# A planned order with another length for a trip through DRAM, and a causal mask that moves from TensorE to GpSimd

## The chip, the cores and the metric

The kernel runs on one core of a Trainium2 chip. The metric is the device time of one execution in microseconds, the median of several runs. A core has five engines with a queue of instructions each: PE (TensorE, matmuls), DVE (VectorE), ACT (ScalarE), POOL (GpSimd) and SP (SyncE, which here only issues DMAs). Each engine takes its instructions in order, and waits at an instruction until the semaphores that it needs have been raised by others.

## The reference

The input x is 8 images of 56 x 56 tokens with 128 channels. Layer 0 is a deformable convolution: per token a depthwise 3x3 convolution gives offsets and weights for nine samples in four channel groups; the samples are summed, projected, and followed by a layer norm, an MLP of 512 and a second layer norm. Layer 1 is causal attention over the 3136 tokens of an image, and then a layer of 64 experts that each choose 8 tokens of an image. The part that the change touches is the attention:

```python
scores = jnp.einsum('bqu,bku->bqk', q, k) / jnp.sqrt(jnp.asarray(T, jnp.float32))
causal = jnp.tril(jnp.ones((T, T), dtype=jnp.float32))
scores = scores + NEG * (1.0 - causal)
attn = jax.nn.softmax(scores, axis=-1)
context = jnp.einsum('bqk,bku->bqu', attn, v)
```

A query sees the keys up to its own place; the softmax subtracts the largest score of its row before the exponential.

## The kernel before, in words

`local_kernel` computes everything. (A general version stands behind a flag for offsets that reach too far; its flag isn't set for these inputs.) The work is cut into 32 groups: 8 images of 4 groups of up to 7 tiles of 128 tokens (896 tokens, or 448 in one group of each image). For each group there is a chain of steps, each a Python generator: `bring` and `prepare` (load and transpose x), `conv`, `plan` (offsets to tap weights), `fetch` (DMA of the neighbourhood, tile g), `weigh` (DVE multiplies g by the taps), `sums` (POOL adds the 25 taps up; for image 0 partly PE), `back`, `project` (the projection, MLP and norms), and then the attention: `norm`, `scores`, `maxes`, `keyed`, `exps`, `attend`, `after`. At the end, behind all groups, stand the experts.

The scores of the attention are computed twice, because the two uses need them the other way round:

- `scores` (L975) makes them with the queries on the partitions (tiles sc). `maxes` (L995) takes each row's maximum on DVE, block by block, and negates it (L1005, L1007). The causal mask is added on the diagonal blocks by a small bf16 matmul of an identity with `maskq` (L990), accumulated into the same PSUM tile.
- The negated maxima stand one to a partition. They have to become one row: ACT issues a DMA of neg to a row in DRAM (L1013, L1017), and SP issues a DMA of that row into the first partition of qT, the transposed queries (L1019). The first channel of the normalised tokens is left free (it holds a one), so that the subtraction of the maximum is part of the next matmul.
- `keyed` (L1040) makes the second scores with the keys on the partitions (tiles st): the matmul at L1047, in pieces of up to 128 keys by 448 queries. A piece that cuts the diagonal has m > 0 columns to mask, and gets a second small matmul with `maskk`, the transposed mask (L1055). There are 803 pieces, and 224 of them are masked. PSUM tiles come from a ring of five (`gen`).
- `exps` (L1060) lets ACT take the exponential of a piece into pe, a ring of three SBUF tiles (L1068).
- `attend` (L1071) multiplies pe by the tokens (tiles av, L1079), accumulated over the keys of a block of queries.

An fp32 matmul is recorded as two instructions, so the 803 pieces appear as 1606.

The order in which the instructions are issued on every engine is fixed when the kernel is built. Each step yields `need(engine, us, ...)`: which engine it uses next, for how long, which ring slots it takes and gives, and with `since` from what time on it may start. These numbers served a planner that isn't part of the file; what it found is written out as the long string `ORDER` (L102 on), one letter a step (x is maxes, t is keyed, e is exps, a is attend, and so on). When the kernel is built, the loop at L1423 only reads a letter and lets that step issue its next instructions; of a `need` it uses the ring slots, for assertions, and nothing else. So an edit of a time in `need` changes nothing by itself; it takes effect through another `ORDER`.

The times that the planner had for the trip of the maxima through DRAM are in these lines of `maxes`: 4.0 us from the issue of the write to the issue of the read, and 2.6 us from there on to the row being in place.

```python
        at = yield need(SP, 0.1, since=at + 4.0)
        nc.sync.dma_start(qT[:1, :N], row[:N].rearrange("(o n) -> o n", o=1))
        yield need(DVE, 0.0, since=at + 2.6)
```

`keyed` and `exps` of a group may begin when `maxes` of that group is done.

Of the kernel before, what the change touches and what calls it, by code (L numbers as in the profile page):

```python
# [9 lines left out]
BF16 = mybir.dt.bfloat16  # L10
# [3 lines left out]
ALU = mybir.AluOpType  # L14
AX = mybir.AxisListType

P = 128
# [57 lines left out]
def need(engine, us, take=None, give=None, since=None, kind=None, when=None, lock=False):  # L75
# [27 lines left out]
    "ppppppbpbkppppbwpwwwpwpwpvkvfvvvvvvvwvpfpccpccwcpwwcbwccfcppccpcccwpcwpccpcbwcvcvcvcvcvcvccv"  # L103
    "cvvwggvvwsvwwvvvvwsvvvgfsvppcccspbccpgppbpscgcpfsscccspcpccvcfsscsvcvcvvcsmvcvcmvfvcvmcvcmvc"
    "vcvmmcvmcvmmvcvmcmvmmgmgvpbmpvgspcmpkscpvmgcfssmsmmmmmpssnpnnnnsfvncvncngpnnsnnncfspncvqqxqv"
    "qgvpgscccfxsscxxgxsvbvcssxvfccsvcgxcctscteftvstvevaevaeavacsvcvcvavocfpcospmccoompoocpcoppoc"
    "opbcbpmggcommoomosoccmococmmpomcmgcsmgmfmpmvcvcvssvcvcsoccccmfsssvcmgcmoscmgsmommfmvmvmcvsgc"
    "vmvcmskmvcmfsvmvmmgmmmcmscmcvvcvmfssvvovooopcgscpcpfssgmpcmgpppmsmmmkmpcfssnmnpgcmspmcmcfncs"
    "smncncmcnmgcscmnvcmfssnmmcmmgnsmnnvbmnvnfvnnvncgcssngcmncmnscnmvvcnfmssmmnmnmvmvnqmgcscvvkcc"
    "xqfsqxcvqmqxxqcmxqxqxcvqcxqcxbsmxqqmqxxmxqvmcmxqmvsvvvvmxfsvgpqpqcmmxgspmxmgxbmskcmpxgpmvcfs"  # L110
    "xtctectcmmcamcmsstesvcmvescvtsesvtsfcvtmtagaaeeameaevasmatatvestvenvtnsntsnnstnsfnentgvaaeae"
    "naeaevgasnvanvmntvnsnmtesctnsageseasfnatnemnacmnmsavonvmmsvnmcsmvnscvnmpcgnbmcpcvcvcoqcqxoxc"
    "qocqqcxoxcqxomxqksmsoqxfqxoqxoqxqxmoqxqxsmqxqmxcqmxsqxcqmmcqxcmxxqmqxoqxmoqxqosmoqqxoxqxqxqs"
    "xosxoqsfxomoxpmxopmgcmspmpmmosmmcxbgscvmsoscmsfocogxpttsetvtvsevaesaecvscmscvokamvfagomtcoet"
    "coamcmomtomseocseacoavostoposestssptfgetetppottsapnnannsanenpnbesnesttpntpgpabpsasfaepeeagpa"
    "etatespttvcstnvnavssavesnctfesangnteanntensvanvenvansvensvanssensfganqqqcqxcxqxqxqcxqxcxqcxq"
    "xcqxqxcqxgqccacaqqcxxcqxqcxqcxxqxqsgxcxqvcscqcsqxsvxqscxsfqxvqcxqccxqcxqsxvmqxmqxsvmxsqsvmsv"
    "qsfxqxtxtcectecsgtettsamaevaescmasvsagcfetcaetcqecqcvcqxqvxcqcxcxqcxmaxacmqcamcxcqgmmqmpobpx"
    "mxqompxopxmoppbmopomoooooxoompkmxotptemttommetmemtmptvavaevtevomvamvomevoavmavaomteetetootot"
    "ooaaemoaoaemeomemoammotmmoommotmoemooomakmaaemtmtmemtmsentnnmntnmsnannmestmtassaseamfetenmaa"  # L120
    "aetesnateanteannaesannanmgsntnstsesaesfnmtngnmnnstneaseqmqxsqxsqxssfqxqgqmamsamxxstxmmssqmsq"
    "xsfemgsxmqmstxkstemtetxsmtgssfaaeceagcsceavmmmcamsacxvsmctsvmsctvsfmgxcteteaesmavavetmcvaesv"
    "ctvsctsectsecftmctctavcaegcaeaecaevacamcapbmcpomocmmgpcmcmocmmtmcpmopccvcevvmvoktmoaootemote"
    "oteomamaematmsotaeomvtmsvemvvtsmvtstoasmaennnansmnasfnnnemeameaamanmmogcmmnmmsnmnccmsncncsnc"
    "snsvsfvovnmnvgnvnvosnvnvonvsvnksmqssqxfqcxmqxqxsqcxqxcmoqxoqmoxqoxsoqmxoqcxsmocxqvsmqsxsmxfq"
    "mcomxvcomvqqcomxqxqmcqxcmxqcxqxqmcxmcxqmcvmxcomvmxvpmcmvcbomovcmvocpvoxcooomcpkcpcxtgmttemet"
    "etpmmtmmsanaennaennnaesnnaagnottesntesoaesnasgnsfonantntteenaeatosteaoetosonoanososeonoasnos"
    "fonagnntnoqeqgxqxsoqoxqoxqoxsoqxosqxosqosxosfqxqxqxqxgmqsmmsqmqxxqssxsasfxagoqoosqoxqxmxqxqs"
    "mxqxsqsxmsqxsfmoxmogcmmsommoccsmomgsposmotbsosmfccgpsemqmqcqxxqkcmcxaxvsqmmqmsmscqmsqcxsfxcq"
    "xqxtxxtegstteaseaesqcsqcssfqxxtxtgxtetaspeaspaecpsaxcaesapsampsfnonnnnxtpeomapsogppmpstbstes"  # L130
    "bposesgftptegptavnaeavasnvnotontnosvenevtsevstnsvmsnfvtvangaeaecaecaoaocoqocooqxmqxocqmqcxxq"
    "xmcqmqcxqoxqxxqxqcoxocqxoqxoqxocomxsogqmmcqsmmocqxmsxqcoxqxqxsgcsxsfqvcvcqxoxtovtesvovtcosva"
    "evsoeavsoscavcsfcovctgoteteaecsavmccttsomtsecmscsooocfcegccpcqpcqcqxcpcxxcbapaemcqkapcxacmgc"
    "apqbmpttexpmxmaepampmtmvtevmvtmexvmvtmvttexvmavmavaeemaemmammammtmmtmememtkmttemamaemmaemsaa"
    "mstmtestetsesttsasfaeaeaeaamsanonmntsotsentmnenanensmasganftmeosnannotgntmeoetosnoanooemonos"
    "onmoomssagsnasfmnmnnmmnonmtnqqsoxqoxemxssogsososfomotqeoqxosqmxqxqxqmxkqxsomxaosmaxmsgossfto"
    "teocomgoscamoceosavooxmststsecsftcgtxetetvmasoavaecsevtevasccsvasevafcvacvmcvtmctctemgeamate"
    "tectetcvptbgcacetacaecmeamaecaapcmommocpcoptmcmocttomopomocotmomvevvcvecovcomakvmaataemotoma"
    "momomsevomvomvosnmeennonansmoansonaosomtntestmoanfeeanamaonnmnomnnsmmgcnmmnommcnscmngcmncovv"
    "cocvvsvcnovmnovkcnvonvoqscosqcxsqsmfxqxvqxqvxpoxqosqpoxqxqmxvqbxsqxmsqmxsqsxsfqxmqxpxqmmqxsm"  # L140
    "xqmpmpxsopmcsqbqscspqmxfxqcmqcpxcxmcxmxocmocmomcommocpommgoxomcpmcccoxtcvoectoctcevoteotooot"
    "oomoakmooaageoeaeamaootomtmomemstogaeotaesoaeotaetonsanteasonensanosnasnfnovmotvmovemnovovmt"
    "vsteteansaesnagsnasnsfntnteotnoaensoooatntseenstnsgtsensftnganeaneqmqxsmqxqxmsxqmqsxmsxsagms"
    "faaqeqqxsxaqxqxsaqxosxqsosqsfxoxqomxqmgsmqmmsqmsqxgsmxsxsfxgmscmoccsoqvckspsxqbpsmqocfxqxqmx"
    "qxqmqxxqxqmmpmsssxmxqmspsmxpsnfnpmnqnonqxnqpxqxqmxnoqnxmqxoqbxnmxnpoxmnonmgnmmnqmxmosoqmpmpq"
    "xxmtxoxtegttsoaetoesgaoeqsesqvsqsfoqomvgovovoocsxccxxqcxscvqcxqssxqxsqsfxcmtgmtamaetesctxakm"
    "somemaocsmaecosmcaogsmcfamomococmvqcqxocqoqmqxxqcmxqxcxqcxqxcqxtoooctcetxectvecgttsqaaevgqev"
    "axsxqeqxsmxcmssvcmscqsfqxmmxvamvxacsvacvttvetstevecasvaesmvxcsatsvfmmgtvxpmtcmscpccsaecbspsm"
    "spetkcppfgcamcaaemetcaemcmpacmmsampbmmpptsgmttstesteseasvsfaevaevavavtvmtvesvaemvatsmeststse"
    "gsftettamgasetetasaeaessaesasfatatnennaennannsnototnegteoetcnntcntcnocancnagnsenonasesnsansf"  # L150
    "eonoaonoonoomonocqmqcxqcxcqxqoxqxqxqsxoqoxoqxosmxooagsmsmosscfommoxcomcomcvscvgcsvcxvssvtcsv"
    "tsfevtexgtectctsctavaevsmvesakmcsacsfacemtgeaevaapcopmtcmmtcbemmpctpocageoceaocpaovctocvmvtm"
    "cevmcevtmvtcvtectvacvaeomaeaecomoaatomatmeoemoammaommotommoototmoemoeeoomaokatmaaomtotommeme"
    "omseanonmnnomnsntonnmeontmotoaaseaeomaanasmossosnfmnmonnmonnmosnomooonsoommonosgcnsmsnsfmnnm"
    "ccngqcvscmvxovovvmvsqkmqcqsxxqxomqxoqxosmoqsxosfqmoxqoxcqmxqxcmqsxcqmcqxcsxqoqxosxmsxqmscfmx"
    "qcmqcqxmxqxmqxqxoxmovxomvmocmmvcovcmmgmmxmcvpbmcpccgxovoctoctectgcpemetkcmtcvacvaecvtepamopp"
    "abemmpammsanmnnpmnoootsteptsnptntmnsensetsmvsfavaveaevaeatantveaetstentntsntnsngassannmfeaea"
    "smanemnamensagnntnsnestsnsgqesfqaaqxsxqxqqxxsqxqxssqxsqxsfqxqxqxtxsgteteteqsqqssxaxssfmexgcm"
    "mqmmsqcmxgcxsmcscqmsqcsxcsfmxgcccscmqcmcsqqkcvmxaxpsmabmsapqmsmqmsfxmxpmxmancqmqsxqxqxmnqxqx"
    "smpqnqsnpsnqxnqxqxsxnqcfxnmnxcqxnnxpcmxoncgmpcncmmpmconmxcbqcgmmcomxtsteomgessqpgqsxpqsxsvxq"  # L160
    "sfxqxqxqxvoaoacootocootceootceoaexmovakmvagtmtetesaeoqmmosqxomqosxoqsxosmqsofxqoxqoxvqxqxqsv"
    "qxxaxsqvosmqsoxsmxsofmgmoqmoqomqxsqmxqxxmsqxmqsxmsxsamgsfmcmmommcgstcmvotvsxtovtsvsomevssfvv"
    "egemamasaeacmootccxktsevtesvtsevstctfavxaevmtemvmamsagsaettseatesteascmscpsfmctcpmgtmpsaaeps"
    "apcbasecepsabpssafgtepettseptgptstvmavaevsavessvaesfgaemaattcevstevaveavcastctesgctesaecsasf"
    "attemeamatactnenoncenctnncntecnacoaenagamcncnomcmscogmmcscmmsvcscomstcfsvtcvtvmvcvcsvcocecsm"
    "ectkesmctsctsoancofoaeomvntevsanmnvtemagnneanseavaoasoonotntgontenasesnesmcafmnmoqqoxcqxoqoc"
    "xocpxqpcqxqxcopbocoqpcqxopcoxaoxtvgcoectcoaceovqovovtotoeteooottxavxmeavmtvemvtvmtaaemxaemaa"
    "emeamxatameommommoamoomotomotoemoeoomoakmattotmeotemmaotmemseaotnonmnnosmnnmonnsamoanooaotte"
    "moeaesmasassfemnanmnamnnmmsnsmmgcnsmmsnsnsfmnnccvncvcmnvgsvvcovcnvsvmnokvmqvsqoxqcxqmxcqxcoq"
    "xcqxvopxqbsmqmoxpqxsqmofxvqxsmqmqxmcqmcmsxqmxqxsqxxqmxqxsqmxsqsxooqfxqxmxpmxpmcmmcoocommcomm"  # L170
    "oxmocppbmocpoocoxcgotoctectctgecaeaeacacgtcmceokmatmtoetemmoemmstotmamnsnoemnootostmootosnos"
    "anmonaeoaesmnaofnatteaevtnevaovaevasnvnanvmntmntnvetsvnengeansaensoasnosnsfpnonpmnoqosqoxoqx"
# [54 lines left out]
def local_kernel(ctx, tc, a, pos, out, flag):  # L227

    nc = tc.nc
# [2150 lines left out]
```

## Time and profile before

| | us |
|---|---|
| median of 3 runs | 3163.42 (3162.01 to 3168.71) |
| the profiled execution | 3155.84 |
| its span, first to last instruction | 3154.0 |

The profiled execution, by engine and by the groups of instructions around the change:

| group | count | busy us | mean of one |
|---|---|---|---|
| L1047 PE, second scores st | 1606 | 664.1 | 0.537 |
| L982 PE, first scores sc | 1594 | 620.1 | 0.523 |
| L1079 PE, av | 1606 | 617.0 | 0.510 |
| L1055 PE, mask of the second scores, 128 and 64 columns | 224 | | 0.219 (median) |
| L1068 ACT, exponentials pe | 803 | 396.5 | 0.504 |
| L1005 DVE, maxima mx | 797 | 442.5 | 0.584 |
| L726 POOL, first addition of the sums | 200 | 690.4 | 3.452 |
| L746, L748 POOL, next additions | 175 each | 317.9, 175.4 | 1.817, 1.002 |
| masks.py:30 POOL, the causal mask by an affine selection, 128x128 | 1 | 0.3 | 0.292 |

Busy time says how long an engine had an instruction in work; "idle before" is the time in which it had none, with what ended the wait. A matmul's record is longer than the distance to the next one[...]; what a matmul costs is read from start to start. The granted clock is the share of TensorE's full speed that the chip allowed in that stretch; its mean over the span is 0.952.

By stage, the profile shows a start (to 158 us) in which the first image is loaded and prepared, a body (158 to 2680 us) in which all steps run interleaved, a stage (to 2997 us) with the attention of the last groups, and the experts (to 3154 us).

### The profile page before, as it was taken

To read this page: it belongs to the slowest core of one execution; us is meant where nothing else is said; L and a number is where in the kernel's file an instruction comes from. 1 tells how busy PE (TensorE), PEld (TensorE's weight loads), DVE (VectorE), ACT (ScalarE), POOL (GpSimd) and SP (SyncE) were. 2 spreads that over 40 slices of the span, in tenths; PEclk is the share of its full clock that TensorE was granted. 3 is DMA by queue.
4 is the path that set the end of the run, shared out by engine and by line. 5 is a ranking of instruction groups with operands and counts; after the bars stand their busy time and mean duration, and the time that the engine had idled before them with its cause. 6 is when DMAs were issued, how large, how long until landed. Compare 5 with 4: busy or idle time off the path is not lost.

```text
span 3154.0 us, 37084 instructions
## 1 busy us (share of the span) xinstructions
PE 2799.6 (89%) x11986; PEld 1655.0 (52%) x11986; DVE 2264.0 (72%) x4101; ACT 1497.9 (47%) x3489; POOL 2235.8 (71%) x2322
## 2 busy tenths in 40 slices
PE   4789899998998989998998999999998999899771
PEld 3666555555555545555555555555554555555331
DVE  6888893788768786677877788678878865467630
ACT  3444445554555435653555545644464455523310
POOL 3767784787678877688877889678977998123453
PEclk9889999999999999999999999999999999999896
DMA  6665443445353444345534445356642553030170
GB/s 175 212 217 187 149 155 76 130 147 191 118 162 116 145 138 170 95 145 166 181 128 106 167 139 190 95 139 187 184 97 87 197 163 112 23 134 12 63 282 26
DMA packets 300849, 442.45 MB, mean 140 GB/s; under 512 B 39812, under 2 KB 153996, under 8 KB 300644
## 3 DMA queue, kind: packets, MB, share of 16 engines
q1 hardware_dynamic: 184612, 382.32, 36.0%
q10 hardware_dynamic: 112768, 51.50, 7.1%
q0 software_dynamic: 3264, 6.15, 0.7%
q8 instruction: 97, 1.59, 0.2%
q14 instruction: 108, 0.88, 0.1%
HBM read 386.27 MB, written 53.81 MB: 140 GB/s over the span
## 4 chain that ended last, share of the span: by engine, by line
PE 65%; DVE 12%; DMA 11%; POOL 6%; issue 3%; ACT 2%; ACTq 0%; SPq 0%; POOLq 0%; DVEq 0%
PE sc L982 16%; PE st L1047 15%; PE av L1079 14%; DMA maxes<-neg 7%; PE ph L857 4%; PE pm L869 3%; DVE g L707 3%; DMA g<-img 2%; DVE pv L568 2%; POOL g L726 1%; DMA qT<-maxes 1%; DVE mx L1005 1%; PE py L843 1%; PE pg L1151 1%; PE pc L1108 1%
## 5 line engine op out<-in xcount | busy, mean ns | idle before, releaser
L707 DVE TENSOR_TENSOR g<-g,tp 128x3200 f32<-128x3200 f32 (+1 forms) x200 | 694.7, 3477 | 100.8 <-DMA g<-img 78.4
L1047 PE MATMUL st<-qT,zT 128*128 128x448 f32 (+8 forms) x1606 | 664.1, 537 | 114.5 <-DMA qT<-maxes 99.5
L726 POOL TENSOR_TENSOR g<-g 128x1536 f32<-128x1536 f32 (+1 forms) x200 | 690.4, 3452 | 94.1 <-DVE g L707 85.6
L1068 ACT ACTIVATE pe<-st 128x448 f32<-128x448 f32 (+8 forms) x803 | 396.5, 504 | 616.8 <-PE st L1047 327.5
L982 PE MATMUL sc<-zT,qT 128*128 128x512 f32 (+4 forms) x1594 | 620.1, 523 | 12.9 <-DVE mx L1005 12.1
L1079 PE MATMUL av<-pe,zk 128*128 128x448 f32 (+8 forms) x1606 | 617.0, 510 | 3.1 <-ACT pe L1068 2.0
L1005 DVE TENSOR_REDUCE mx<-sc 128x1 f32<-128x512 f32 (+6 forms) x797 | 442.5, 584 | 140.3 <-PE sc L982 97.5
L1047 PEld LDWEIGHTS st<-qT,zT 128*128 128x128 f32 (+1 forms) x1606 | 289.9, 199 | 358.4 <-issue 246.5
L1079 PEld LDWEIGHTS av<-pe,zk 128*128 128x128 f32 (+1 forms) x1606 | 288.3, 192 | 235.1 <-issue 182.2
L982 PEld LDWEIGHTS sc<-zT,qT 128*128 128x128 f32 x1594 | 275.9, 188 | 255.1 <-issue 122.5
L568 DVE SCALAR_TENSOR_TENSOR pv<-xg,dw,pv 128x448 f32<-128x448 f32 x448 | 307.6, 687 | 49.2 <-ACT pv L565 38.1
L746 POOL TENSOR_TENSOR g<-g 128x768 f32<-128x768 f32 (+1 forms) x175 | 317.9, 1817 | 8.9
L857 PE MATMUL ph<-xT,fc 128*128 128x512 f32 (+2 forms) x448 | 214.5, 572 | 23.6 <-DVE xT L795 23.1
L861 ACT ACTIVATE hid<-ph,b_fc 128x512 f32<-128x512 f32 (+2 forms) x224 | 140.7, 634 | 159.9 <-PE ph L857 152.8
L659 POOL TENSOR_TENSOR taps<-taps,a 128x252 f32<-128x252 f32 (+1 forms) x288 | 190.3, 661 | 17.8
L649 POOL TENSOR_TENSOR a<-w 128x756 f32<-128x756 f32 (+1 forms) x96 | 135.9, 1415 | 83.5 <-DVE w L640 76.8
L869 PE MATMUL pm<-fc,hid 128*128 128x128 f32 x1600 | 194.4, 279 | 0.0
L869 PEld LDWEIGHTS pm<-fc,hid 128*128 128x128 f32 x1600 | 183.5, 192 | 11.8 <-issue 11.6
L748 POOL TENSOR_TENSOR g<-g 128x384 f32<-128x384 f32 (+1 forms) x175 | 175.4, 1002 | 11.1
L1285 POOL TENSOR_TENSOR share<-share,part 128x512 f32<-128x512 f32 x56 | 71.0, 1268 | 133.4 <-DVE part L1275 132.7
L778 POOL TENSOR_SCALAR ssb<-ssb 128x4 f32<-128x4 f32 (+1 forms) x56 | 11.2, 199 | 179.1 <-ACT ub L776 161.9
L857 PEld LDWEIGHTS ph<-xT,fc 128*128 128x128 f32 x448 | 78.9, 197 | 82.2 <-issue 32.6
(263 smaller groups left out, 4150.8 us busy)
## 6 DMA issues: line engine op xcount, KB each, us to landing
g<-img SPq DMA_DIRECT2D x192, 1600.0 KB
w1t<-in_L_ffn_weight_dram SPq DMA_DIRECT2D x32, 512.0 KB
w2t<-in_L_ffn_weight_dram SPq DMA_DIRECT2D x32, 512.0 KB
xin<-in_x_dram SPq DMA_DIRECT2D x56, 224.0 KB
xTd<-xc ACTq DMA_DIRECT2D x56, 224.0 KB
img<-st ACTq DMA_DIRECT2D x112, 112.0 KB
out_dram<-t ACTq DMA_DIRECT2D x24, 448.0 KB
od<-o ACTq DMA_DIRECT2D x24, 448.0 KB
```

Source lines behind the costliest of these rows:

```text
L568: nc.vector.scalar_tensor_tensor(p3, src, dw[:, k : k + 1], p3, op0=ALU.mult, op1=ALU.add)
L659: nc.gpsimd.tensor_add(dst, dst, a5[:, :nt, kx])
L707: nc.vector.tensor_mul(g3, g3, tp[:n, lt % 4].unsqueeze(2).to_broadcast([n, NTAP * NG, 32]))
L726: nc.gpsimd.tensor_add(g[:n, : 12 * C], g[:n, : 12 * C], g[:n, 12 * C : 24 * C])
L746: nc.gpsimd.tensor_add(g[:n, : 6 * C], g[:n, : 6 * C], g[:n, 6 * C : 12 * C])
L857: nc.tensor.matmul(ph[:, :n], fc1[:, f * P : (f + 1) * P], xT[:, :n], start=True, stop=True)
L869: nc.tensor.matmul(four(pm, m)[:, i, :], hid[:, f, i * P : (i + 1) * P], fc2[:, f, :], start=False, stop=i == m - 1 and f == 3,)
L982: nc.tensor.matmul(pp[:w, :n], qT[:, i * P : i * P + w], zTs[b, g][:, k0 : k0 + n], start=True, stop=not diagonal,)
L1005: nc.vector.tensor_reduce(mx[:w, i, j : j + 1], pp[:w, :n], AX.X, ALU.max)
L1047: nc.tensor.matmul(pp[:w, :n], zTs[b, g][:, j * P : j * P + w], qT[:, u * CH + q0 : (u + 1) * CH], start=True, stop=m <= 0,)
L1068: nc.scalar.activation(pe[:w, :n], pp[:w, :n], AF.Exp, scale=SCALE)
L1079: nc.tensor.matmul(av[:, q0:CH], zs[b, g][:w, j, :], pe[:w, : CH - q0], start=first, stop=last)
```

## The change

Four things are edited.

1. In `maxes` the times of the trip through DRAM become 12.0 and 3.5 us for 4.0 and 2.6.
2. In `project` the cost of a DVE instruction becomes 0.345 us for 0.32.
3. The second scores lose the mask matmul; `maskk` and its transposition at the start go. Instead `exps` lets GpSimd set the masked exponentials to zero, after ACT has written them: `affine_select` keeps an element of row p and column c where m0 + c − p is at least 0. `maskq`, the mask of the first scores, stays.
4. `ORDER` is another string, in which `exps` has 1027 letters for 803 (one more for each of the 224 masked pieces) and `settle` 17 for 19; all others have as many as before, at other places.

```diff
@@ -100,126 +100,128 @@
 ORDER = (
...
@@ -408,7 +410,6 @@
-    maskk = cst.tile([P, P], BF16, tag="maskk", name="maskk")
@@ -467,11 +468,6 @@
         nc.vector.tensor_copy(maskq, mask)
-        yield need(PE, 0.2, take="gen")
-        pt = gen("pt_mask")
-        nc.tensor.transpose(pt[:, :P], mask, ident)
-        yield need(ACT, 0.3, give="gen")
-        nc.scalar.copy(maskk, pt[:, :P])
@@ -883,7 +879,7 @@
-                yield need(DVE, 0.32)
+                yield need(DVE, 0.345)
@@ -1015,9 +1011,9 @@
-        at = yield need(SP, 0.1, since=at + 4.0)
+        at = yield need(SP, 0.1, since=at + 12.0)
         nc.sync.dma_start(qT[:1, :N], row[:N].rearrange("(o n) -> o n", o=1))
-        yield need(DVE, 0.0, since=at + 2.6)
+        yield need(DVE, 0.0, since=at + 3.5)
@@ -1041,7 +1037,7 @@
-            at = yield need(PE, 0.00168 * n + 0.056 * (m > 0), take="gen", since=since)
+            at = yield need(PE, 0.00168 * n, take="gen", since=since)
@@ -1049,12 +1045,8 @@
-                stop=m <= 0,
-            )
-            if m > 0:
-                nc.tensor.matmul(
-                    pp[:w, :m], identb[:w, :w], maskk[:w, m0 : m0 + m], start=False, stop=True
-                )
+                stop=True,
+            )
@@ -1066,6 +1058,18 @@
             nc.scalar.activation(pe[:w, :n], pp[:w, :n], AF.Exp, scale=SCALE)
+            if m > 0:
+
+                at = yield need(POOL, 0.2 + 0.0013 * m)
+                nc.gpsimd.affine_select(
+                    out=pe[:w, :m],
+                    in_=pe[:w, :m],
+                    compare_op=ALU.is_ge,
+                    fill=0.0,
+                    base=m0,
+                    pattern=[[1, m]],
+                    channel_multiplier=-1,
+                )
             expd[b, s, u, g, j] = pe, at
```

## The prediction

> **What bounds the kernel now.** I read the page's busy shares first, then the table of windows by stage, the waits of PE, the chain of waits, and last the timeline around one of the waits.
>
> ```profile
> PE 2799.6 (89%) x11986; PEld 1655.0 (52%) x11986; DVE 2264.0 (72%) x4101; ACT 1497.9 (47%) x3489; POOL 2235.8 (71%) x2322
> 158.00:2680.00 2522.00, 2356.01 (x9629) 1384.55 (x9629) 1917.24 (x3266) 1314.61 (x3078) 1986.65 (x2015) 0.97 0.47 146
> 2680.00:2997.00 317.00, 280.61 (x1008) 153.62 (x1007) 194.25 (x537) 111.75 (x253) 88.02 (x103) 0.93 0.18 59
> ```
>
> The columns of a window are its length, then busy time of PE, weight loads, DVE, ACT and POOL, then the granted PE clock, DMA share and GB/s. From 158 to 2680 us PE is busy for 2356 of 2522 us (93%), POOL for 79%, DVE for 76%. PE is the bound of that stage, and of the next (89%); it can win only its 166 + 36 us of idle time, its slow-clock time, or less work.
>
> ```profile
> PE st L1047 <- DMA qT<-maxes: 99.5, 19, 7.3
> PE ph L857 <- DVE xT L795: 23.1, 14, 6.4
> PE sc L982 <- DVE mx L1005: 12.1, 10, 2.8
> SPq L1019 <- DMA maxes<-neg: 601.2, 34, 80.0
> ```
>
> Total, times and longest in us. Half of PE's idle time in the body is one wait: the first matmul of the second scores (st) of 19 of the 32 groups waits for the maxima to come back from DRAM. No other wait reaches a quarter of it. The last line is SP's queue, which stands on the same round trip. The chain of waits shows its anatomy in one group:
>
> ```profile
> 356.80 0.17 DVE neg L1007
> 356.97 0.02 issue
> 356.99 13.66 DMA maxes<-neg
> ...
> 370.79 2.12 DMA qT<-maxes
> 372.92 0.14 issue
> 373.05 5.07 PE st L1047 x8
> ```
>
> From the last maximum to the first st: 16.1 us. Over the 19 groups I find mostly 13 to 16 us: 10 to 15 for the write, about 2 for the read. The order of before was made with 4.0 and 2.6 us for the two legs.
>
> The wait costs more than its length. Windows of 8 us from the start of the first st, two after a wait and one of a group without:
>
> ```profile
> 289.26:297.26 8.00, 8.00 (x20) 3.79 (x21) 4.65 (x4) 4.61 (x9) 2.38 (x1) 0.67 1.02 391
> 1384.61:1392.61 8.00, 8.00 (x22) 4.77 (x23) 4.45 (x7) 2.52 (x9) 4.57 (x7) 0.65 0.06 10
> 1589.10:1597.10 8.00, 8.00 (x31) 4.55 (x30) 7.09 (x21) 2.85 (x6) 7.33 (x14) 1.00 0.35 136
> ```
>
> The granted clock is the third number from the right: about two thirds after a wait, full without one. I took this window for all 19: 18 lie between 0.65 and 0.80, one is at 1.00, and (1 − clock) × 8 us adds up to 40.7 us of PE time. Of the 13 groups that did not wait for the maxima, 12 show 1.00. So the round trip costs 99.5 + 40.7 = 140 us of PE.
>
> **What the Trainium skill says.** "TensorE: Matmul & The Clock Gate", Part 1: the array falls to half rate after an idle window of about 3.4 us and needs as long of busy time to recover. The trace agrees: waits of 4 to 7 us are followed by about 4 to 5 us at 0.5. "DMA: Bandwidth & Descriptors", Rules for kernel authors: a strided last dimension becomes one descriptor per element, and a DMA should be issued early and waited on late. The write is 896 single floats; the trace has 10 to 15 us for it and about 2 for the contiguous read-back. "GPSIMD Engine Reference", § 4.1: one-input operations run at about VectorE's rate there; the trace has one such selection of 128x128, at 0.29 us.
>
> **The change part by part.**
>
> 1. *The numbers in need() (12.0 and 3.5 for 4.0 and 2.6, 0.345 for 0.32) and the new ORDER.* The numbers do nothing when the kernel is built; only ORDER acts. I compared the two built orders. For each group I added the PE work that stands between its last first-score matmul and its first st, pricing a matmul by its start-to-start time in the trace (448 columns in fp32: 0.75 to 0.80 us). Before, the groups that wait have 8 to 10 us there. Needed are about 15.3 us (one maximum and its negation, then about 14). The shortfalls of before sum to 115 us by this count, where the trace has 99.5; so the yardstick reads about 15% high. In the new order most groups have 17 to 30 us; short are the groups 0, 1, 2, 13, 18, 25 and 29 (10.7, 11.9, 9.5, 7.7, 14.6, 6.0, 8.6 us), in sum 38 us. Share left: 38/115 = 0.33. Waits: −99.5 × 0.67 = −66.5 us. Slow clock: −40.7 × 0.67 = −27.3 us. What is late next is what fills those gaps: it is pulled from elsewhere, but the total is the same, and PE has no other large wait.
>
> SP's queue: the read of the maxima now stands behind up to 11 more loads (mostly g, xT) than before, so it no longer blocks the g loads while it waits. DVE waits 78.4 us for g in all; a gain of 0 to 15 us, and I take 0 because that time isn't PE's.
>
> 2. *The mask matmul of the second scores (224 of them) and its weight load leave PE.* Its record lasts 0.22 us, but the next matmul starts 0.06 us later:
>
> ```profile
> 298.00 0.22 PE L1055 MATMUL st<-maskk,identb 128*128 128x128 bf16 x1
> 298.06 0.76 PE L1047 MATMUL st<-qT,zT 128*128 128x320 f32 x2
> ```
>
> So 224 × 0.056 = −12.6 us, not 224 × 0.22. The transpose of the mask at the start goes too (7.2 us of waiting on POOL at 46 to 54 us); PE is only 60% busy up to 158 us, so 0, at best −7.
>
> 3. *224 selections on POOL.* 224 × 0.3 = 67 us more on POOL. Over the body that raises it from 79% to about 84% once the body is 90 us shorter; it still has room, DVE too (79%). The price is the new wait: av of a masked piece now waits exp → selection, and the selection stands in POOL's queue behind additions of 3.45, 1.82 and 1.0 us. Behind a selection that waits for its exponential stand the sums of the sampled taps (which free the g buffers), the powers of the norms (ACT waits for those) and gate's gathers; behind av stands all of PE's queue. In the new order the PE work between st and av of a masked piece has a median of 4.0 us; 5 of 224 have under 1.5 us, which is what exp (0.54), the selection (0.3) and handing over need, and 66 have under 3. If POOL is caught inside an addition, the mean rest of it, weighted by POOL's rows, is about 0.85 us. A stall of about 0.7 us in one of eight pieces is 20 us; if POOL runs late as often as DVE waits for g (28 times, up to 8.4 us) it is more. Bounds: 0 (the slack hides it) to 67 us (0.3 us each). I take +20.
>
> Also, pe has three buffers and one is held longer; exp already waits 188 us for av, hidden by PE's other work: inside the bounds above. ACT loads a table 16 times more often in the new order (180 for 164), at 1.28 us: 20 us on an engine at 47%; 0, at worst 10.
>
> 4. *Where the work stands.* In the new order PE has 261 us of work left after the last project matmul, where it had 240: front work is done earlier by about 35 us of PE time, and more is left for the stage from 2680 us, where PE has 36 us of idle time and POOL almost nothing to do. I count 0, ±15.
>
> Sum: −66.5 − 27.3 − 12.6 + 20 = −86 us on the profiled execution's 3155.84 us (span 3154.0), which gives 3069. The median of the runs shown, 3163.42, lies 7.6 us above it: 3077 us.
>
> **Rivals.** *The full gain*: the order hides nearly all waits, selections included: −(140 × 0.85) − 12.6 − 10 (SP) = −142, so 3022. For it: the medians of slack, the better place of SP's read. Against: seven groups stay short by count.
>
> *POOL and DVE take over*: front work is limited by POOL, whose 86% from 2366 to 2680 us is already close, and PE waits for sums and selections instead: +67 instead of +20, so 3124. For it: in-order queues at 84%. Against: POOL's idle time of before is mostly waiting for others.
>
> *Slower*: one mechanism, POOL's queue in front of av. The gain without it is 106 us, so it decides at 106/224 = 0.48 us of PE time per selection. At 0.65 us (146 us) the time is 3204. Half the pieces would have to stall for 1.3 us, slow clock included. Against: only 66 of 224 have under 3 us of cover; for it: a POOL that runs late would hit four pieces in a row.
>
> *The round trip isn't what the new numbers say*: if the write took over 20 us when g loads run beside it, the gaps of 17 to 25 us would be short again. The slowest write in front of a wait took 14.7 us; I put this under the second rival.
>
> **How the numbers follow.** Forecast (3045 to 3105): 0.55. Full gain (below 3045): 0.15. POOL takes over (3105 to 3157): 0.18. Slower than 0.2%: 0.09. Within 0.2% (6 us, about what a measurement of this kernel tells from no change): 0.03. Faster: 0.55 + 0.15 + 0.18 = 0.88. The range 3020 to 3140 takes in most of the second and third cases and leaves out about 0.2.
>
> **What would show it.** Right: the wait of st on qT<-maxes near 33 us in about seven groups; PE's clock above 0.96; no L1055 records; a mask selection row on POOL of about 67 us; waits of av on POOL of some 20 us. Wrong: av waits for pe on POOL above 60 us, PE's busy share in the body below 93%, or waits on the maxima still above 60 us; then the order, or the count that I made on it, did not do what I read from it.

## The result, and the profile after

| | before | after |
|---|---|---|
| median of 10 runs each, us | 3165.89 (3161.24 to 3173.32) | 3140.52 (3125.55 to 3148.61) |
| ratio | 1 | 0.9916 [0.9899, 0.9933] |
| span of the profiled execution, us | 3154.0 | 3141.3 |

The kernel became faster, by 25 us where 86 were forecast. First the page of the kernel after: its row of busy times and the row of the selections.

```profile
PE 2780.0 (88%) x11761; PEld 1644.0 (52%) x11761; DVE 2264.1 (72%) x4101; ACT 1516.4 (48%) x3504; POOL 2295.7 (73%) x2546
...
L1064 POOL TENSOR_SCALAR_AFFINE_SELECT pe<-pe 128x128 f32<-128x128 f32 (+1 forms) x224 | 61.5, 282 | 147.1 <-ACT pe L1060 145.5
```

Then its windows (columns as above: length, busy PE, weight loads, DVE, ACT, POOL, clock, DMA share, GB/s). The second one is the stage with the attention of the last groups. It runs 15 us into the experts, whose first matmul starts at 2968.9 us; the window 2680 to 2997 of before runs 4 us into them.

```profile
158.00:2680.00 2522.00, 2367.64 (x9601) 1394.79 (x9601) 1922.22 (x3311) 1353.83 (x3160) 2047.88 (x2231) 0.97 0.47 146
2680.00:2984.00 304.00, 250.48 (x884) 131.85 (x882) 185.98 (x504) 95.21 (x196) 95.24 (x119) 0.91 0.24 75
```

And its waits of PE, DVE, POOL and SP (total, times, longest, in us):

```profile
PE ptg L729 <- POOL g L722: 37.2, 13, 17.0
PE st L1043 <- DMA qT<-maxes: 35.4, 5, 25.6
PE ph L853 <- DVE xT L791: 16.6, 9, 5.8
...
PE av L1083 <- POOL pe L1064: 1.3, 2, 1.1
...
DVE g L703 <- DMA g<-img: 96.9, 25, 10.8
...
POOL pe L1064 <- ACT pe L1060: 145.5, 104, 24.6
...
SPq L1015 <- DMA maxes<-neg: 367.4, 30, 84.3
```

The edit did what it says: the wait for the maxima fell from 99.5 to 35.4 us, and 25.6 of that is one wait. `av` hardly ever waits for a selection. But PE is idle as long as before, and the body's clock is 0.97 as before. From 2680 us to the first matmul of the experts PE is idle for 48 us, where it was 36.

Where the time went is seen best in a balance of PE. From the span's start to PE's last matmul the time is work at full clock, plus what the slow clock adds, plus idle time; after the last matmul every kernel here has 60 us more. I take the slow-clock part from the records of the granted clock: the sum of (1 − clock) × busy time. Each column is one profiled execution. The two kernels without the trip are experiments told below.

| us | before | after | before, no trip (x3) | after, no trip (x6) |
|---|---|---|---|---|
| work of PE at full clock | 2719.0 | 2702.1 | 2710.0 | 2695.9 |
| slow clock | 80.6 | 77.8 | 36.1 | 60.3 |
| idle | 294.3 | 301.1 | 174.2 | 204.6 |
| of this, st waiting for the maxima | 99.5 | 35.4 | 0 | 0 |
| span | 3154.0 | 3141.3 | 2980.6 | 3021.0 |

Read across, the trip costs 173 us in the old order (3154.0 − 2980.6) and 120 in the new one: it became 53 us cheaper. Read between the last two columns, everything else (the order and the mask edits) became 40 us dearer. The difference is the 12.7 us of the two profiled spans.

The columns don't all come from one chip and are one execution each, so these sizes are rough. By the ratios to before, each on its own chip, the trip costs 5.3% in the old order and 2.7% in the new one, and everything else became 1.8% dearer, which is 58 us. The direction is not in doubt: on one chip the new order is 50 us dearer without a trip (x10 and x9) and 44 us dearer with a short one (x7 and x8). The kernel after was profiled a second time, in another batch (x13): slow clock 75.2, idle 286.1, of this 35.4 for the maxima, span 3120.9.

### The profile page after: what moved, and what is told of

Its sections match the earlier page's. It is cut to its first block, busy times and chain, and to the rows that moved or that the text cites. A ratio compares the mean times of both kernels' runs of the same rounds, so it can differ in the third digit from the quotient of the medians.

```text
span 3141.3 us, 36798 instructions
## 1 busy us (share of the span) xinstructions
PE 2780.0 (88%) x11761; PEld 1644.0 (52%) x11761; DVE 2264.1 (72%) x4101; ACT 1516.4 (48%) x3504; POOL 2295.7 (73%) x2546
## 4 chain that ended last, share of the span: by engine, by line
PE 61%; POOL 13%; DVE 10%; DMA 10%; issue 4%; ACT 2%; ACTq 0%; SPq 0%; POOLq 0%; DVEq 0%
PE av L1083 14%; PE st L1043 13%; PE sc L978 13%; DMA g<-img 6%; PE ph L853 4%; PE pm L865 4%; POOL g L722 3%; DVE g L703 3%; POOL g L742 2%; DMA maxes<-neg 1%; PE py L839 1%; PE pg L1155 1%; DVE mx L1001 1%; POOL taps L655 1%; PE ptg L729 1%
## 5 line engine op out<-in xcount | busy, mean ns | idle before, releaser
L703 DVE TENSOR_TENSOR g<-g,tp 128x3200 f32<-128x3200 f32 (+1 forms) x200 | 695.2, 3477 | 115.2 <-DMA g<-img 96.9
L1043 PE MATMUL st<-qT,zT 128*128 128x448 f32 (+8 forms) x1606 | 625.9, 515 | 53.3 <-DMA qT<-maxes 35.4
L978 PE MATMUL sc<-zT,qT 128*128 128x512 f32 (+4 forms) x1594 | 635.0, 528 | 18.5 <-DVE mx L1001 13.3
L1083 PE MATMUL av<-pe,zk 128*128 128x448 f32 (+8 forms) x1606 | 625.5, 510 | 13.0 <-DVE avs L1092 9.6
L1064 POOL TENSOR_SCALAR_AFFINE_SELECT pe<-pe 128x128 f32<-128x128 f32 (+1 forms) x224 | 61.5, 282 | 147.1 <-ACT pe L1060 145.5
L1092 DVE COPY avs<-av 128x448 f32<-128x448 f32 x56 | 34.8, 621 | 139.0 <-PE av L1083 139.0
```

The source lines that it names most:

```text
L703: nc.vector.tensor_mul(g3, g3, tp[:n, lt % 4].unsqueeze(2).to_broadcast([n, NTAP * NG, 32]))
L978: nc.tensor.matmul(pp[:w, :n], qT[:, i * P : i * P + w], zTs[b, g][:, k0 : k0 + n], start=True, stop=not diagonal,)
L1043: nc.tensor.matmul(pp[:w, :n], zTs[b, g][:, j * P : j * P + w], qT[:, u * CH + q0 : (u + 1) * CH], start=True, stop=True,)
L1083: nc.tensor.matmul(av[:, q0:CH], zs[b, g][:w, j, :], pe[:w, : CH - q0], start=first, stop=last)
```

## The experiments

Chips differ: the kernel before took 3154, 3128, 3133 and 3155 us on those of the four batches (x1 to x4, x5 to x8, x9 to x12, x13 to x16). So I compare kernels of one batch where a per cent or less matters. Each kernel is given with its median, and its ratio to before on its own chip with the 95% interval.

**x3, x4: the trip and the selections in the old order.** Edits of the kernel before; x3 takes out the write and the read, x4 the mask matmul, for the selection:

```diff
-        nc.scalar.dma_start(
-            row[: full * P].rearrange("(i p) -> p i", p=P), neg[:, :full]
-        )
-        if part:
-            nc.scalar.dma_start(row[full * P : N].rearrange("(p i) -> p i", i=1), neg[:part, full : full + 1])
...
-        nc.sync.dma_start(qT[:1, :N], row[:N].rearrange("(o n) -> o n", o=1))
```

> The kernel before, without the DMA of the maxima to DRAM and without the read of it; the second scores are not shifted by the row's maximum. Order and all else as before. The working of the prediction (the waits for the trip and the slow clock after them come back in full, 99.5 + 40.7 us): 3166 - 140 = 3026 us. Theory B (a part of it is given back, since PE then runs into waits on DVE, ACT and POOL that its own lateness had hidden): PE's waits on DVE rise from 94 to 120 us or more, and the time is 3070 to 3110.

Measured for x3: 2984.3 us, 0.9466 [0.9445, 0.9488]. It is faster than either theory had it: the trip is worth 170 us by runs on one chip, not the 140 of the prediction.

```diff
-                stop=m <= 0,
-            )
-            if m > 0:
-                nc.tensor.matmul(
-                    pp[:w, :m], identb[:w, :w], maskk[:w, m0 : m0 + m], start=False, stop=True
-                )
+                stop=True,
+            )
...
+            if m > 0:
+                nc.gpsimd.affine_select(
+                    out=pe[:w, :m],
+                    in_=pe[:w, :m],
+                    compare_op=ALU.is_ge,
+                    fill=0.0,
+                    base=m0,
+                    pattern=[[1, m]],
+                    channel_multiplier=-1,
+                )
```

> The kernel before, with the mask matmul of the second scores replaced by the selection on POOL, each right behind its exponential in the order; the order is otherwise the one of before. Theory A: the selections cost more than the mask matmul saves (12.6 us): 3180 us or more. Theory B (selections are nearly free, hidden behind POOL's idle time): 3150 to 3165. In both the waits of PE on the maxima stay near 100 us.

Measured for x4: 3204.3 us, 1.0149 [1.0124, 1.0173], 50 us slower than before, as theory A expected. The waits of PE and POOL in x4:

```profile
PE av L1085 <- POOL pe L1066: 50.1, 45, 6.0
...
POOL pe L1066 <- ACT pe L1064: 215.4, 85, 30.1
```

This is the mechanism of the "slower" rival. Put into the order of before, the selections wait in POOL's queue and PE waits for them 45 times; with the 13 us of mask matmuls saved, they cost 63 us, or 0.28 us each. In the kernel after the same wait is 1.3 us. The new order makes room for them; the edit without the order loses.

**x1, x2: two suspects in the kernel after.** In x1, SP issues the experts' first 20 weight loads only after the read of group 29 (`give_up` no longer issues them; the loop that reads `ORDER` does, once `maxes` has passed group 29). In x2 the selections are left out:

```diff
-        for e in range(0, EFIRST, EG):
-            weights(e, ep, "w1t", "w2t", EFIRST // EG)
+        experts["late"] = True
...
+            if experts.get("late") and lines["maxes"].at > 29:
+                experts.pop("late")
+                for e in range(0, EFIRST, EG):
+                    weights(e, experts["pool"], "w1t", "w2t", EFIRST // EG)
```

x2:

```diff
-                nc.gpsimd.affine_select(
-                    out=pe[:w, :m],
-                    in_=pe[:w, :m],
...
-                )
```

> The changed kernel with one edit: SP issues the first 20 weight loads of the experts only after the maxima of group 29 have been read back. Theory C (in the changed order the read of the maxima of group 29 stands in SP's queue behind those loads, and this costs PE the 25.6 us wait): the wait of st on qT<-maxes falls from 35 to about 10 us, and the time from 3140 to about 3112, ratio to before near 0.983. Rival (PE finds another wait in the same place, or the later loads make the experts wait): within 8 us of 3140.

> The changed kernel without the 224 selections; the second scores are left without a mask, so the output isn't the reference's. Order and all else as changed. Theory A (POOL, held at the selections for the exponentials, delays sums, g and through them DVE and PE): POOL is freed of 145 us of waits, PE's waits on DVE fall from 135 to below 110 us, and the time from 3140 to 3105 or less. Theory B (PE, no longer held at the trip, meets the lateness that DVE has anyway): waits on DVE stay near 135 us and the time within 8 us of 3140.

Measured: x1 3113.7 us, 0.9882 [0.9853, 0.9910]; x2 3110.5 us, 0.9867 [0.9827, 0.9906]. In x1 the wait on the maxima fell to 11.8 us, as its theory had it. Beside the kernel after (0.9916, another chip) both look 0.3 to 0.5% better, but that is no more than chips scatter. Both were run again, with the kernel after beside them (x13 to x16, below).

**x5, x6: half of the trip, and the new order without it.** x5 is before with the write kept and the read dropped; x6 is after with both dropped, by the diff of x3 (the maxima are not subtracted in either).

```diff
-        nc.sync.dma_start(qT[:1, :N], row[:N].rearrange("(o n) -> o n", o=1))
```

> The kernel before with the write of the maxima to DRAM and without the read, so that neither SP nor PE waits for the trip; the second scores are not shifted by the row's maximum. Without both DMAs the time was 0.947 of before, 170 us less. Theory D (the 900 packets of 4 bytes of each write slow the g loads beside them, which took 216 ns a packet there for 114 elsewhere, and DVE waits for g): a good part of the 30 us beyond the 140 of the wait comes back, ratio 0.952 to 0.956. Rival (the 30 us were SP's queue standing at the read): ratio stays at 0.947 within 0.002.

> The changed kernel without the write and the read of the maxima; the second scores are not shifted by the row's maximum. If the new order had hidden the trip and only the selections (17 us) and the tail (11 us) were in its way, it would now be near the old order without a trip: ratio to before 0.95 to 0.96. Theory E (the new order pays for the trip with its own arrangement, so that taking the trip out gives little): ratio 0.975 to 0.985, with PE's waits on DVE and ACT still above 170 us.

**x7, x8: the same trip in longer packets**, in the old and in the new order. The Trainium skill says (VectorE: DVE Perf Modes, The three transpose paths) that DVE transposes blocks of 32 x 32 only. That is enough here: with neg as a tile of 128 x 32, each partition then holds 32 maxima of one tile, and the write is 128 runs of 128 bytes.

```diff
-    rows_ = [indram(f"maxes{j}", [GT * P]) for j in range(2)]
+    rows_ = [indram(f"maxes{j}", [P * 32]) for j in range(2)]
...
-                neg = wk.tile([P, GT], F32, tag="neg", name=f"neg{nm}", bufs=2)
+                neg = wk.tile([P, 32], F32, tag="neg", name=f"neg{nm}")
+                nc.vector.memset(neg, 0.0)
...
+        turn = wk.tile([P, 32], F32, tag="turn", name=f"turn{nm}")
+        nc.vector.transpose(turn, neg)
...
+        nc.scalar.dma_start(row.rearrange("(p i) -> p i", i=32), turn)
...
+        nc.sync.dma_start(
+            qT[:1, : nt * P].rearrange("o (i r p) -> o i r p", r=4, p=32),
+            row.rearrange("(o r i p) -> o i r p", o=1, r=4, p=32)[:, :nt],
+        )
```

> The kernel before with the maxima turned by one DVE transpose of 32x32 blocks, so that the write has 128 packets of 128 bytes for 896 of 4 bytes; the read takes them in runs of 128 bytes. Order as before. If the length of the trip is its element-wise write, it falls from 14 to about 5 us, which the old order's 6.6 us cover: PE's wait on the maxima below 15 us and a ratio of 0.945 to 0.955. If the trip is long for another reason (the landing itself), the wait stays above 60 us and the ratio above 0.975.

> The changed kernel with the same short trip. Theory E: 0.975 to 0.985, little better than the changed kernel, since its order waits out a trip that is no longer there. Theory D alone (packets of 4 bytes beside the g loads were what kept the new order from its gain): 0.96 or less.

Measured in this batch (before 3127.9 us):

| | us | ratio |
|---|---|---|
| x5, before, write only | 3030.3 | 0.9691 [0.9675, 0.9707] |
| x7, before, short trip | 2988.4 | 0.9555 [0.9539, 0.9571] |
| x6, after, no trip | 3020.2 | 0.9650 [0.9630, 0.9670] |
| x8, after, short trip | 3032.4 | 0.9691 [0.9675, 0.9707] |

x7 came out at the edge of what was expected for it. The others lie outside both of their expected ranges: x5 above both, x6 and x8 between them.

x5 against x7 is the telling pair. In x5 nobody waits for the maxima, and it is still 42 us slower than x7, which makes the whole trip and whose PE never waits for it. The pages' counts of packets (the pieces in which the profile records a DMA), x5 and then x7:

```profile
DMA packets 300783, 442.33 MB, mean 146 GB/s; under 512 B 39780, under 2 KB 153956, under 8 KB 300580
```

```profile
DMA packets 280666, 442.88 MB, mean 148 GB/s; under 512 B 19660, under 2 KB 133836, under 8 KB 280460
```

And what DVE waits for the loads of the neighbourhoods, in the same order:

```profile
DVE g L707 <- DMA g<-img: 65.9, 29, 9.2
```

```profile
DVE g L707 <- DMA g<-img: 30.7, 19, 4.8
```

Twenty thousand fewer small packets, and DVE's wait for g halves. The same line in before, with the whole trip, and in x6, without one:

```profile
DVE g L707 <- DMA g<-img: 78.4, 28, 8.4
```

```profile
DVE g L703 <- DMA g<-img: 20.4, 14, 4.3
```

The packets themselves show why: in before, a 2560-byte packet of a g load takes 216 ns on average in the 12 us after a write of maxima is issued, and 114 ns at other times. In x7 it takes 111 ns in the 12 us after its write, so the slow packets come from the single floats, and not from other work that falls into the same time. So the trip has a second price that no wait on the maxima shows: while 896 single floats are written, the g loads beside them run at half speed, DVE waits for g, and PE for what follows. The Trainium skill (DMA: Bandwidth & Descriptors, Specifications) gives 512 bytes as the smallest transfer at line rate, below which the DMA engine reads, modifies and writes. These runs agree that small packets are bad, but 128 bytes, also below that, cost the g loads nothing here (the 111 ns of x7).

x6 against x7 says something else: the new order *without* a trip is 32 us slower than the old order *with* the short one.

**x9, x10: the two orders alone.** After and before without trip and without any mask of the second scores, so that only the order is different (with the mask's set-up at the start, which x10 still has). x9 has the diffs of x3 and x2 on after, x10 on before the diff of x3 and the mask matmul taken out as in x4.

> The kernel after without the write and the read of the maxima (so the maxima are not subtracted) and without the 224 selections (so the second scores have no causal mask): the new order and nothing else of the change. Theory, the new order itself is slower once the trip is out: the kernel after without the trip stood at 0.965 of before, the selections are worth some 17 us (0.005), so 0.958 to 0.962, and this is 1.2 to 1.8% of before above the next run. Rival, the 60 us between the two kernels without the trip come from the selections: within 0.5% of the next run, about 0.945.

> The kernel before without the write and the read of the maxima (they are not subtracted) and without the 224 mask matmuls of the second scores (no causal mask there): the old order and nothing else. Both theories: the kernel before without the trip (0.9466) less 12.6 us (0.004), so 0.942 to 0.947. PE's last matmul of project near 2590 us, and some 215 us from there to the first matmul of the experts; with the new order (the run above) the theory of the order has 2600 and 245 us, its rival 215 us there too.

Measured (before 3133.4 us): x9 3033.0, 0.9674 [0.9648, 0.9700]; x10 2982.9, 0.9519 [0.9503, 0.9535]. The new order is 50 us slower for practically the same instructions on the same chip, 1.6% of before, which is inside the range of the theory. From the last matmul of `project` to the experts x9 takes 246.2 us and x10 213.5, near the 245 and 215 that were expected. Both ratios lie above the expected ones. For x10 the faster before of this chip accounts for it (its time is that of x3); for x9 it doesn't, since before was faster still where x6 ran. In part it is the experts: they took 173.8 us in x9 and 172.0 in x10, but 162.3 in x6 and 161.4 in x3. Windows of x9 and x10 (start, body, and the stage up to the experts with their first 11 to 12 us), x9 first:

```profile
0.00:158.00 158.00, 94.84 (x558) 81.06 (x559) 119.83 (x192) 54.34 (x117) 86.68 (x132) 0.83 0.59 191
158.00:2600.00 2442.00, 2359.42 (x9654) 1393.15 (x9654) 1924.94 (x3331) 1363.91 (x3183) 2000.59 (x2038) 0.98 0.44 152
2600.00:2872.00 272.00, 241.16 (x841) 126.26 (x839) 180.38 (x482) 86.97 (x180) 86.10 (x89) 0.92 0.22 77
```

```profile
0.00:158.00 158.00, 94.36 (x586) 80.13 (x586) 115.94 (x203) 58.85 (x133) 88.78 (x136) 0.95 0.62 205
158.00:2600.00 2442.00, 2378.36 (x9783) 1407.04 (x9784) 1941.40 (x3386) 1361.04 (x3200) 2000.67 (x2042) 0.99 0.44 151
2600.00:2820.00 220.00, 196.18 (x684) 102.53 (x682) 160.33 (x417) 64.25 (x131) 79.74 (x79) 0.93 0.24 85
```

In the body x9 gets 19 us less of PE work done, and at a lower clock; in the next stage it has more work left and more idle time (31 for 24 us). The balance of PE splits the difference of the spans (52.7 us): work −0.7, slow clock +29.2, idle +24.2. So the order that was planned with a long trip costs more by itself; with a trip that is short, or gone, nothing comes back for it. Which of the planner's new numbers makes it so (the trip, the dearer DVE instruction, the places for the selections) isn't shown: no order made with a part of them was run.

**x11, x12.** x11 is x8 with the weight loads later (the edits of x8 and x1 together). x12 is after with the mask matmul in place of the selection: the new order, and no other part of the change (but `maskk` is made at the start by a second selection on POOL, where before transposed the first):

```diff
...
-                stop=True,
+                stop=m <= 0,
...
+            if m > 0:
+                nc.tensor.matmul(
+                    pp[:w, :m], identb[:w, :w], maskk[:w, m0 : m0 + m], start=False, stop=True
+                )
...
-                nc.gpsimd.affine_select(
...
-                )
```

> The kernel after, with the maxima turned by DVE in blocks of 32 x 32 so that their way through DRAM is 128 packets of 128 bytes, and with the first 20 weight loads of the experts issued by SP after the read of the maxima of group 29. Theory, the 18 us that PE still waits for the row of group 29 with the short trip are the weight loads ahead of its read: they go, 0.960 to 0.965, and the stretch from the last matmul of project to the experts falls from 258 to some 240 us. Rival, other work of that stage ends at the same time: 0.967 to 0.971. By neither theory does it reach the 0.9555 that the old order has with the short trip.

> The new order with the causal mask of the second scores added by the small matmul on PE, as before, and no selection: the order alone. Theory, selections cost some 16 us and the mask matmuls 12.6 us, so the two edits nearly cancel: 0.988 to 0.993, and PE's start-to-start distance after a mask matmul stays near 0.06 us. Rival, the small matmuls hide in PE's other waits in this order (DVE, POOL), so the selections are a plain loss: 0.986 to 0.988. Second rival, the order has no place for the small matmuls and needs the selections: 0.994 or more.

Measured: x11 3035.6 us, 0.9690 [0.9674, 0.9707]; x12 3114.6 us, 0.9943 [0.9926, 0.9959]. x11 took the time of x8, outside the range of its theory and inside that of its rival. The traces say something else than the rival, though. The wait of 18.3 us that x8 had is gone, and the stretch from the last matmul of `project` to the experts fell from 257.9 to 246.3 us, so most of that wait came out of this stretch. But the experts took 173.9 us for 160.8. All four kernels of this batch show that, old order or new (171 to 174 us, and 161 to 163 in every other profile but that of after); PE stands there for up to 5 us at a matmul with nothing in the profile that it waits for. So x11 and x8, on two chips, don't tell what the weights cost with a short trip. The same holds for x12: it gave no answer by itself, its experts took 170.6 us, and the same kernel on another chip (x16, 161.0 us) has a ratio 0.4% lower.

**x13 to x16: the small terms on one chip.** The edits are those of x2, x1 and x12; x13 is the kernel after.

> The kernel after itself, beside the three runs below on one chip. Both theories: ratio to before 0.988 to 0.994; the absolute time goes with the chip's time of before[...].

> The kernel after without the 224 selections (no causal mask of the second scores). Theory S, the selections cost some 16 us through POOL's late sums, as forecast: 0.4 to 0.6% below the kernel after on this chip. Rival, they cost nothing (with the trip out, the new order took 3020 us with them and 3033 without, on two chips) and the difference seen before was that of the chips: within 0.25% of the kernel after on this chip.

> The kernel after with the 20 first expert weight loads issued after the read of the maxima of group 29. Theory W, the 25 us wait of group 29 is a loss of its own: 0.3 to 0.7% below the kernel after on this chip. Rival, other work ends at the same time there (with the short trip, the same edit moved nothing: 3032 and 3036 us): within 0.25%.

> The new order with the mask on PE and no selection: the order alone. If theory S holds (selections some 16 us, mask matmuls 13 to 17 us of PE), within 0.25% of the kernel after on this chip. If the selections are free: 0.3 to 0.6% above the kernel after. If PE's waits cover the small matmuls: 0.4% or more below it.

| before 3155.5 us | us | ratio |
|---|---|---|
| x13, after | 3123.8 | 0.9911 [0.9890, 0.9931] |
| x14, no selections | 3121.6 | 0.9883 [0.9864, 0.9902] |
| x15, weight loads later | 3107.9 | 0.9853 [0.9838, 0.9868] |
| x16, mask on PE, no selections | 3124.5 | 0.9903 [0.9887, 0.9920] |

The intervals of x13 and x14 overlap: the selections cost between 2 us (medians) and 9 us (ratios), which isn't told from nothing. x16 lies on x13: the two mask edits cancel, and the order alone, by its shorter waits for the trip, makes the gain. The weight loads are a loss of their own, as their theory had it: 16 us. From x13 to x15 the stretch from the last matmul of `project` to the experts falls from 263.6 to 246.3 us.

What happens there is seen in the chain of waits of the kernel after. `give_up` issues 20 weight loads on SP when the last `project` is done; in the new order that is just ahead of the read of group 29, which stands behind them in SP's queue:

```profile
2718.48 16.97 DMA maxes<-neg
2735.45 0.02 issue
2735.46 0.37 SPq L1415
...
2736.39 5.85 DMA w1t<-in_L_ffn_weight_dram
...
2742.31 8.82 DMA qT<-maxes
2751.12 0.14 issue
2751.26 3.21 PE st L1043 x4
```

The read is issued 7 us after the write has landed, and then takes 8.8 us beside the weights, where it took 2. In x15 the wait has nearly gone:

```profile
PE st L1043 <- DMA qT<-maxes: 9.4, 4, 5.6
```

**The best version.** x7 beats both kernels: 0.9555 of before, where the change came to 0.99. It keeps the old order and the mask on PE. The new order on top of it (x8) takes back 44 us. DVE pays 9.5 us for the turn (32 transposes of 212 ns and 32 clearings of 85 ns), on an engine at 75%.

## Why the prediction was wrong

1. *The waits on the maxima, −66.5 us*: −64.1 was measured, but that it fits so well is luck. Of the 35.4 us left, four waits are 9.8 us in all, where the count had some 27 for the groups without group 29 (31.4 us short, times 99.5/115). Group 29 was short by 6.7 us in the count (15.3 − 8.6) and waits 25.6, because its read stands behind the weight loads. The prediction looked at what is ahead of the read in SP's queue, but only at g and xT.

2. *The slow clock, −27.3 us*: right for the trip, wrong for the kernel. By the balance the trip's share went from 44.5 us (80.6 − 36.1) to 17.5 (77.8 − 60.3), a gain of 27.0. The new order, with the mask edits, brought 24.2 us of its own (60.3 − 36.1), so that only 2.8 us show. One profile is rough here too: x2 and x14, the same kernel, have 79.4 and 90.1 us of it.

3. *"What is late next is what fills those gaps: it is pulled from elsewhere, but the total is the same, and PE has no other large wait."* This is the step that failed. Idle time on anything but the maxima went from 194.8 to 265.7 us, +71 (250.7 in x13, +56), where the prediction had 0. It is in no single large wait: by the sums over the list of waits, PE waits for DVE 135 us where it was 94, for ACT 69 (60) and for POOL 41 (31), and 11 us are stops without a releaser in the profile (0.5 in x13). The prediction looked for a large wait and found none; the 194.8 us of small ones, twice the wait on the maxima, it took as fixed without a run. Two parts of the rise are separated by the runs:
   - the order with the mask edits, +30 idle (x6 against x3); the order alone, +24 on one chip (x9 against x10);
   - the trip's indirect price, which rose from 20.6 to 61.1 us of idle time (idle without the trip and without the waits on the maxima taken off: 294.3 − 99.5 − 174.2, and 301.1 − 35.4 − 204.6; with x13 for after, 46.1). With the short trip it is gone in the new order too: x8 is idle for 219.0 us, 18.3 of them on the maxima, so 200.7 against x6's 204.6. So it comes from the single floats and what they do to others' transfers. More g packets run in the 12 us after a write in the new order (8617, where it was 5703), and DVE's wait for g rose from 78.4 to 96.9 us; with the short trip it is 28.3 (x8). How much of the 61 us goes through g and how much through other loads wasn't separated.

   Planned as a longer wait, a write of 896 single floats still sends 896 packets. The prediction measured the trip by who waits for it, 140 us; taken out, it is worth 170. It asked whether the g loads would lengthen the write, and not what the write does to the g loads.

4. *SP's queue and the g loads, a gain of 0 to 15, taken as 0*: SP's wait at the read did fall, from 601.2 to 367.4 us, but DVE's wait for g rose, for the reason just given.

5. *The mask matmuls, −12.6 us*: right as work of PE (−16.9; without the trip −13.5, x10 against x3). As time, x16 against x14 gives 3 to 6 us. Most of it fell into waits: x16 has 20.8 us more work on PE than x14, and 18.2 us less idle time.

6. *The selections, +20 us*: too dear; 2 to 9 us, and not told from nothing. The cover counted from the order (a median of 4.0 us) was enough: `av` waits 1.3 us. POOL is busy for 81% of the body, where 84 were forecast. What rose was POOL's own waiting for exponentials (145.5 us), mostly covered. x4 shows that the fear had its place: with the old order it costs 63.

7. *Where the work stands, 0 ± 15*: outside the bounds. The last `project` matmul came 66.7 us earlier (2771.5, then 2704.8 us), but from there to the first matmul of the experts it took 264.1 us for 221.6: 21 us more of work, which had been counted, and 21 us more of idle time, which had not. About 17 of these are the weight loads in front of group 29 (x13 against x15). The experts took 172.4 us for 160.9 in this profile, but nothing shows that the change did it: they took 162.5 us in x13, the same kernel, and 172.0 in x10, in the old order.

The rival "POOL and DVE take over", at 3124 us, was nearest in size, and in naming DVE and POOL as what PE waits for. Its mechanism, the selections, isn't it. (The prediction's 3204 us for the third rival should be 3203 by its own sum; nothing rests on it.)

What stays open: which of the new order's thousands of moved steps make its 24 us of idle time and 29 us of slow clock. Nine of the latter are in the start, where the clock is 0.83 in x9 and 0.95 in x10; but x1 and x15, one kernel on two chips, differ by 7 us there too. No run takes the order apart.

## What to carry to other kernels

A wait on a slow transfer has two prices: what stands behind the wait, and what the transfer does to others while it runs. Hiding it by planning further ahead removes the first, can raise the second, and here cost time elsewhere in the order; before doing that, take the transfer out altogether to see what it is worth, and look for a form of it that is cheap. When a static order is made anew, price the order by itself: run both orders with the disputed work removed from both, on one chip. And loads that the planner doesn't know, here 20 weight loads in SP's queue, land in front of something.

## What the runs showed of the hardware

- Writes of 4-byte packets slow their neighbours: a 2560-byte packet takes 216 ns beside them, 114 otherwise, and 111 beside writes of 128 bytes. The write-only trip costs 42 us more than the whole trip in packets of 128 bytes.
- Chips differ by 1.2% for the kernel before (3128 to 3166 us), while the old order without the trip or with the short one took 2984, 2988 and 2983 us on three of them. These are three different kernels, one chip each, so it is a hint and no proof that what differs between chips is the trip. Something else differs as well: the experts took 171 to 174 us in all four profiles of one batch and 172.4 in that of after, and 161 to 163 in all others.
- One profiled execution is a sample: x2 and x14 are the same kernel, and PE was idle for 270 us in one profile and 285 in the other. A difference of 15 us between two profiles needed runs on one chip to mean anything.
